# A four-layer image kernel: layer 3 writes its output with channels on partitions, its residual added by an identity product and its shifts as ScalarE's bias

## The chip, the cores and the metric

The kernel runs on one core of a Trainium2 chip. A core has TensorE (PE, with its weight loads PEld), VectorE (DVE), ScalarE (ACT) and GpSimd (POOL), and queues that issue DMAs. The metric is the device time of one execution in microseconds, lower is better. All arithmetic is in float32 except the small bf16 rows named below.

## The reference

The input `x` has 16 images of 64 x 64 tokens and 256 channels. Four layers follow each other, each as `x = x + layer(_gn(x))`, where `_gn` is a group norm over 32 groups of channels:

- Layer 0 replaces each normalized token by the nearest of 1024 code vectors.
- Layer 1 is attention with a sigmoid along each row of the image.
- Layer 2 computes a gate for each token, from a softmax over all pairs of the 4096 tokens of rank-one scores, and multiplies the token by it.
- Layer 3 is linear attention. What matters here is its end:

```python
out = jnp.einsum('bhde,bhdn->bhen', context, q)
...
out = jnp.einsum('bxyh,hc->bxyc', out, w_out) + b_out
mu = jnp.mean(out, axis=-1, keepdims=True)
var = jnp.mean(jnp.square(out - mu), axis=-1, keepdims=True)
out = (out - mu) * jax.lax.rsqrt(var + LN_EPS) * gamma + beta
```

and the sum with the layer's input, which is the result.

## The kernel before, in words

The tokens of an image are worked on in 8 chunks of 512 (`NCHUNK`, `CW`), a chunk being 4 tiles (`CH`) of 128 tokens. Between the layers the activations lie in DRAM with the channels on the partitions: a chunk is 128 partitions x 2 channel halves (`NK`) x 512 tokens.

Each layer is a generator for each image: `stage1` searches the codes, `layer1` is the row attention, `rows2`, `stage2` and `gate2` make layer 2, `stage3` is layer 3. Their steps are merged in an order written out by hand: each stage has a start and a length in units of one image (`LAG4`, `LEN3` for layer 3), and a heap picks the next step. So several images are in flight, each in another layer, and all engines work on all of them. Within that, the scheduler of the language fixes the order on each engine by priority; blocks under `tc.high_priority` are drawn forward.

PSUM is used through two pools: four single banks of 512 columns (`bank`, pool `ps_m`), shared by nearly everything, and two double ones for the search and layer 1.

`stage3` runs over the chunks twice. In the first pass it reads `xk`, makes keys, queries and values (`pk`, `pqv`) and adds up the context; the queries go to DRAM. Then it forms `wctx` from the context, `w_out` and `gamma`. In the second pass each chunk reads its queries back (`fetch`), gets the variance by a product with the Gram matrix (`form`, `variance`), scales the queries by the deviation (`deviate`), and computes the output.

That last step treats a chunk in two halves of two token tiles. For each half a PSUM tile `px` of 128 tokens x 2 x 256 channels takes, in one accumulation, four transposes of the residual `xt` (L902), two products of the scaled queries with `wctx` (L908), and one bf16 product with `x_row` that adds the shifts of each channel to all tokens (L912). ScalarE copies it to `y` (L913), and a chunk's `y` goes out with the tokens on the partitions (L923, L926), in pieces of 256 channels.

The shifts are `xm_`, two columns of 128 channels made in `gate2` (L688: `beta` less the mean that was added there). To add them to tokens on partitions they are needed as a row. `put_row` makes one with a weight function, `by_identity` (L173 to L178): ScalarE copies the column three times (L148), `busy` issues `idle` products that nobody reads (L135), the product with the identity gives a row (L176), and the row is split into three bf16 parts with two more copies, two small products and a last copy (L156 to L158). It is called once an image, in the first chunk of layer 3, with `idle=8` (L789). `h_row` and `qv_row` of layers 1 and 3 are made the same way, without the idle products.

The tag `u4` has two buffers, used by `qv` in the first pass and `y` in the second; `xb` has four, for every chunk that layer 3, `rows2` and the first statistics read.

Of the kernel before, what the change touches and what calls it, by code (L numbers as in the profile page):

```python
# [9 lines left out]
F32 = mybir.dt.float32  # L10
BF16 = mybir.dt.bfloat16
U32 = mybir.dt.uint32
AF = mybir.ActivationFunctionType
# [3 lines left out]
P = 128  # L17
C = 256
NK = C // P
TOK = 4096  # L20
NT = TOK // P
CH = 4
NCHUNK = NT // CH
CW = CH * P
# [19 lines left out]
def kernel(  # L44
# [7 lines left out]
    nc = tc.nc  # L52
# [10 lines left out]
    s3p = ctx.enter_context(tc.tile_pool(name="s3p", bufs=2))  # L63
# [6 lines left out]
    def bank(name):  # L70
        return ps_m.tile([P, 512], F32, tag="pm", name=name)
# [5 lines left out]
    ident = const.tile([P, P], F32, name="ident")  # L77
# [38 lines left out]
    ones3 = const.tile([P, P], BF16, name="ones3")  # L116
# [10 lines left out]
    def row_tile(name):  # L127
        t = const.tile([P, C], BF16, name=name)
        nc.gpsimd.memset(t, 0.0)
        return t  # L130
# [6 lines left out]
                skip_group_check=True,  # L137
            )

    h_row, qv_row, x_row = row_tile("h_row"), row_tile("qv_row"), row_tile("x_row")  # L140

    def twice(row):
        return row.unsqueeze(1).to_broadcast([P, 2, C])

    def put_row(dst, v, weight, tag, plus=None, idle=0):

        v3 = small.tile([P, NK, PARTS], F32, tag="v3", name=f"v3_{tag}")
        nc.scalar.copy(v3, v.unsqueeze(2).to_broadcast([P, NK, PARTS]))  # L148
        pb = bank(f"prow_{tag}")
        busy(pb, idle)  # L150
        row = pb[:PARTS, :C]
        weight(row, v3, plus)

        for n in range(PARTS - 1):
            top = small.tile([PARTS, C], BF16, tag="ptop", name=f"top_{tag}_{n}", bufs=1)
            nc.scalar.copy(top, row)  # L156
            nc.tensor.matmul(row, lhsT=below[:, n, :], rhs=top, start=False, stop=True, skip_group_check=True)
        nc.scalar.copy(dst[0:PARTS, :], row)  # L158

    def by_weight(w):  # L160
# [9 lines left out]
                    skip_group_check=True,  # L170
                )
        return make

    def by_identity(out, v3, plus):
        for k in range(NK):
            nc.tensor.matmul(  # L176
                out[:, k * P : (k + 1) * P], lhsT=v3[:, k, :], rhs=ident, start=(k == 0), stop=(k == NK - 1),
                skip_group_check=True,  # L178
            )


    e_raw = s2p.tile([P, NK, CODES], F32, tag="x0b", name="e_raw", bufs=2)
# [6 lines left out]
    for hf in range(2):  # L189
        pe = bank(f"pe_{hf}")  # L190
        for k in range(NK):
            nc.tensor.matmul(
                pe, lhsT=neg_mat, rhs=e_sq[:, k, hf * 512 : (hf + 1) * 512],
                start=(k == 0), stop=(k == NK - 1),
# [54 lines left out]
    for n in range(2):  # L249
        t = const.tile([P, CH, 2, ROW], F32, name=f"blk_{n}")  # L250
# [4 lines left out]
    for n in range(4):  # L255
        t = const.tile([P, 8], F32, name=f"m8_{n}")
# [459 lines left out]

    def stage3(b):
        tag = f"s3_{b}"
        dst = out[b].rearrange("(t p) c -> p t c", p=P)
        x3 = x3_d.pop(b)  # L720
        scale, nmean, xm_ = norm3.pop(b)
        wk_n = wts.tile([P, NK, P], F32, tag="wk_n", name=f"wk_{tag}")
# [35 lines left out]
        for ch in range(NCHUNK):  # L758
            xt = xb.tile([P, NK, CW], F32, tag="xb", name=f"xk_{tag}_{ch}")
            nc.sync.dma_start(out=xt, in_=x3[ch])  # L760
            if ch > 0:
                normalize(ch - 1)
            pk = bank(f"pk_{tag}_{ch}")
            for k in range(NK):
                nc.tensor.matmul(pk, lhsT=wk_n[:, k, :], rhs=xt[:, k, :], start=(k == 0), stop=(k == NK - 1))  # L765

            now = nkm[:, ch : ch + 1]
            nc.vector.tensor_reduce(now, pk, AX.X, ALU.max, negate=True)
            if ch > 0:
                last = nkm[:, ch - 1 : ch]  # L770
                nc.vector.tensor_scalar(now, now, last, None, ALU.min)
                nc.scalar.activation(al[:, ch : ch + 1], last, AF.Exp, scale=-1.0, bias=now)
            kx = s3p.tile([P, CW], F32, tag="v2", name=f"kx_{tag}_{ch}", bufs=7)
            nc.scalar.activation(kx, pk, AF.Exp, bias=now, accum_out=ks[:, ch : ch + 1])
            qv = s3p.tile([P, CH, 2, P], F32, tag="u4", name=f"qv_{tag}_{ch}")
            qvs[ch] = qv
            for pr in range(CH // 2):
                pqv = bank(f"pqv_{tag}_{ch}_{pr}").rearrange("p (j n) -> p j n", j=2)
                for j in range(2):
                    t = 2 * pr + j  # L780
                    for k in range(NK):
                        nc.tensor.matmul(  # L782
                            pqv[:, j, :], lhsT=xt[:, k, t * P : (t + 1) * P], rhs=wqv_n[:, k, :],
                            start=(j == 0 and k == 0), stop=False, skip_group_check=True,
                        )
                nc.tensor.matmul(pqv, lhsT=ones3, rhs=twice(qv_row), start=False, stop=True, skip_group_check=True)
                nc.scalar.copy(qv[:, 2 * pr : 2 * pr + 2, :, :].rearrange("p j s n -> p j (s n)"), pqv)
            if ch == 0:
                put_row(x_row, xm_, by_identity, f"x_{tag}", idle=8)  # L789
            yield 5  # L790
            pkt = bank(f"pkt_{tag}_{ch}")
            for t in range(CH):
                nc.tensor.transpose(pkt[:, t * P : (t + 1) * P], kx[:, t * P : (t + 1) * P], ident)
            ek = s3p.tile([P, CH, P], F32, tag="v2", name=f"ek_{tag}_{ch}", bufs=7)
            nc.scalar.copy(ek.rearrange("p t d -> p (t d)"), pkt)
            if ch > 0:
                queries(ch - 1)

            q4 = qv[:, :, 0, :].rearrange("p t (h d) -> p t h d", d=DH)
            qm = small.tile([P, CH, HEADS], F32, tag="qm", name=f"qm_{tag}_{ch}")  # L800
            nc.vector.tensor_reduce(qm, q4, AX.X, ALU.max)  # L801
            nc.gpsimd.tensor_tensor(q4, q4, qm.unsqueeze(3).to_broadcast([P, CH, HEADS, DH]), ALU.subtract)  # L802
            nc.scalar.activation(qv[:, :, 0, :], qv[:, :, 0, :], AF.Exp)

            pc = bank(f"pc_{tag}_{ch}")
            for t in range(CH):
                nc.tensor.matmul(pc[:, :P], lhsT=ek[:, t, :], rhs=qv[:, t, 1, :], start=(t == 0), stop=(t == CH - 1))
            if ch > 0:
                nc.vector.scalar_tensor_tensor(
                    ctxa, ctxa, al[:, ch : ch + 1], pc[:, :P], op0=ALU.mult, op1=ALU.add  # L810
                )
            else:
                nc.vector.tensor_copy(ctxa, pc[:, :P])
            yield 5
# [15 lines left out]
        with tc.high_priority(offset=URGENT):  # L830
# [8 lines left out]
            wctx = wts.tile([P, 2, C], F32, tag="wctx", name=f"wctx_{tag}")  # L839
# [50 lines left out]
        for ch in range(NCHUNK):  # L890
            xt = xb.tile([P, NK, CW], F32, tag="xb", name=f"xo_{tag}_{ch}")
            nc.sync.dma_start(out=xt, in_=x3[ch])
            qT = qs[ch]
            y = s3p.tile([P, CH, C], F32, tag="u4", name=f"y_{tag}_{ch}")
            for pr in range(2):
                if pr == 1 and ch + 1 < NCHUNK:
                    deviate(ch + 1)
                px = bank(f"pxo_{tag}_{ch}_{pr}").rearrange("p (j c) -> p j c", c=C)
                for j in range(2):
                    t = 2 * pr + j  # L900
                    for k in range(NK):
                        nc.tensor.matmul(  # L902
                            px[:, j, k * P : (k + 1) * P], lhsT=xt[:, k, t * P : (t + 1) * P], rhs=ident,
                            is_transpose=True, start=(j == 0 and k == 0), stop=False, skip_group_check=True,
                        )
                for j in range(2):
                    t = 2 * pr + j
                    nc.tensor.matmul(  # L908
                        px[:, j, :], lhsT=qT[:, t * P : (t + 1) * P], rhs=wctx[:, 1, :], start=False, stop=False,
                        skip_group_check=True,  # L910
                    )
                nc.tensor.matmul(px, lhsT=ones3, rhs=twice(x_row), start=False, stop=True, skip_group_check=True)  # L912
                nc.scalar.copy(y[:, 2 * pr : 2 * pr + 2, :], px)  # L913
                if pr == 0:
                    if ch + 2 < NCHUNK:
                        form(ch + 2)
                    if ch + 3 < NCHUNK:
                        fetch(ch + 3)
                else:
                    if ch + 2 < NCHUNK:  # L920
                        variance(ch + 2)
                    if before is not None:
                        nc.sync.dma_start(out=dst[:, (ch - 1) * CH : ch * CH, :], in_=before)  # L923
                yield 3
            before = y
        nc.sync.dma_start(out=dst[:, TOK // P - CH :, :], in_=before)  # L926

# [75 lines left out]
```

## Time and profile before

| | us |
|---|---|
| median of 3 runs | 5682.38 (5680.2 to 5684.69) |
| the profiled execution | 5674.06 |
| its span, first to last instruction | 5672.1 |
| busy: PE, PEld | 5162.0, 3189.6 |
| busy: DVE, ACT, POOL | 5049.3, 4571.1, 1801.5 |
| mean granted clock of TensorE | 0.962 |

The span has 76,096 instructions. A line such as `L902 PE MATMUL pxo_s<-ident,xo_s 128*128 128x128 f32` names the line of the kernel, the engine, the operation, the tile written and those read (the program's names, shortened) and the size. A float32 product shows as two records, a transpose or a bf16 product as one. The records of successive matmuls overlap, so that the distance from one start to the next says what a matmul occupies, and its duration says more than that. The DMA lines count packets: 521,365 in the run, with 1059.26 MB.

### The profile page before, as it was taken

What the parts mean: (1) busy time and instruction counts of PE and PEld (TensorE: products, weight loads), DVE (VectorE), ACT (ScalarE), POOL (GpSimd) and SP (SyncE); (2) the same over time, 40 slices, a digit from 0 to 9 for tenths busy, and PEclk for the clock granted to TensorE, in tenths of its full rate; (3) what the DMA queues carried; (4) which work ended last, traced back from release to release, by engine and by line L of the source; (5) the groups of instructions that cost most, each with busy time, mean ns of one, the idle gap of its engine ahead of it and who ended that gap; (6) DMA issues with size and microseconds to landing.
All of it is one profiled execution on the core that took longest, in us unless ns stands there. A gap on an engine that the chain in (4) does not pass through costs nothing.

```text
span 5672.1 us, 76096 instructions
## 1 busy us (share of the span) xinstructions
PE 5162.0 (91%) x26927; PEld 3189.6 (56%) x26927; DVE 5049.3 (89%) x7186; ACT 4571.1 (81%) x6642; POOL 1801.5 (32%) x1076
## 2 busy tenths in 40 slices
PE   7977889989999999999999999999999999987788
PEld 3534446545656566565655656565565656564556
DVE  7589799899999999999999999999999999988882
ACT  4468589888989898888978888898888879887873
POOL 2223234323333333334333333333333333321221
PEclk9988999999999999999999999999999999998889
DMA  8553744655665757566575656657575675745543
GB/s 254 174 178 84 232 115 144 214 163 185 196 198 175 224 159 236 171 211 198 185 234 155 216 185 200 210 173 236 160 224 183 201 219 156 222 149 176 200 157 119
DMA packets 521365, 1059.26 MB, mean 187 GB/s; under 512 B 52504, under 2 KB 266392, under 8 KB 512792
## 3 DMA queue, kind: packets, MB, share of 16 engines
q1 hardware_dynamic: 406288, 885.11, 46.5%
q0 software_dynamic: 73728, 67.14, 8.3%
q10 hardware_dynamic: 40968, 102.13, 4.6%
q8 instruction: 214, 3.51, 0.3%
q14 instruction: 167, 1.37, 0.1%
HBM read 751.18 MB, written 303.04 MB: 186 GB/s over the span
## 4 chain that ended last, share of the span: by engine, by line
PE 46%; DVE 17%; ACT 16%; issue 6%; DMA 5%; POOL 4%; SPq 0%; ACTq 0%; DVEq 0%; POOLq 0%
PE pd_s L403 14%; ACT ex_s L645 7%; DVE ex_s L648 7%; PE ph_l L493 4%; PE pxo_s L908 3%; PE pqv_s L782 3%; PE po_l L533 2%; PE pk_s L765 2%; ACT nn_s L398 2%; POOL qv_s L802 2%; PE pz_s L857 2%; DVE i_s L414 2%; DVE nn_s L409 2%; PE pxo_s L902 2%; PE pvr_s L865 2%
## 5 line engine op out<-in xcount | busy, mean ns | idle before, releaser
L648 DVE CUSTOM_DVE_ANT_0 ex_s<-ex_s,x2b 128x2048 f32<-128x2048 f32 x1024 | 2360.4, 2312 | 77.6 <-ACT ex_s L645 74.6
L645 ACT ACTIVATE ex_s<-x0b,nmax_s,x_r 128x2048 f32<-128x2048 f32 x1024 | 2138.6, 2089 | 40.7 <-DVE num_s L648 30.5
L403 PE MATMUL pd_s<-e,xn_s 128*128 128x512 f32 x4096 | 1971.1, 614 | 43.9 <-DVE m L409 27.9
L415 POOL DMA_INDIRECT xc_s<-in_emb_rows,i_s x512 | 1113.7, 2175 | 1852.7 <-DVE i_s L414 1337.5
L403 PEld LDWEIGHTS pd_s<-e,xn_s 128*128 128x128 f32 x4096 | 745.8, 195 | 778.8 <-issue 669.1
L409 DVE CUSTOM_DVE_ANT_0 nn_s<-pd_s,nn_s 128x1024 f32<-128x1024 f32 x512 | 619.9, 1212 | 113.5 <-PE pd_s L403 63.0
L414 DVE FIND_INDEX8 i_s<-m,nn_s 128x8 uint32<-128x1024 f32 x512 | 622.9, 1217 | 0.0
L398 ACT ACTIVATE nn_s<-ne,nx_s 128x1024 f32<-128x1024 f32 x512 | 582.5, 1143 | 33.1 <-DVE nx_s L369 18.7
L493 PE MATMUL ph_l<-wh_l,xt_l 128*128 128x256 f32 x2048 | 519.6, 390 | 28.7 <-DVE m L409 16.9
L782 PE MATMUL pqv_s<-wqv_s,xk_s 128*128 128x256 f32 x2048 | 489.3, 381 | 0.0
L493 PEld LDWEIGHTS ph_l<-wh_l,xt_l 128*128 128x128 f32 x2048 | 379.7, 192 | 138.9 <-issue 69.0
L782 PEld LDWEIGHTS pqv_s<-wqv_s,xk_s 128*128 128x128 f32 x2048 | 389.1, 191 | 120.6 <-issue 59.7
L802 POOL TENSOR_TENSOR qv_s<-qv_s,qm_s 128x512 f32<-128x512 f32 x128 | 221.6, 1731 | 662.6 <-DVE qm_s L801 363.2
L868 POOL TENSOR_TENSOR lrs_s<-lrs_s,mhalf 128x4 f32<-128x4 f32 x128 | 178.0, 1391 | 677.2 <-ACT lrs_s L867 663.3
L756 POOL TENSOR_TENSOR qv_s<-qv_s,qd_s 128x512 f32<-128x512 f32 x128 | 214.4, 1675 | 249.0 <-DVE qd_s L755 132.0
L533 PE MATMUL po_l<-blk,h_l 128*128 128x128 f32 x2048 | 282.1, 288 | 3.0 <-DVE m L409 1.5
L533 PEld LDWEIGHTS po_l<-blk,h_l 128*128 128x128 f32 x2048 | 260.6, 200 | 41.1 <-issue 24.5
L908 PE MATMUL pxo_s<-wctx_s,qo_s 128*128 128x256 f32 x1024 | 269.2, 386 | 2.2 <-DVE qo_s L876 2.2
L765 PE MATMUL pk_s<-xk_s,wk_s 128*128 128x512 f32 x512 | 256.0, 620 | 1.0 <-DMA xk_s<-x_g 0.9
L913 ACT COPY y_s<-pxo_s 128x512 f32<-128x512 f32 x256 | 147.5, 580 | 132.4 <-PE pxo_s L912 116.0
L378 PE MATMUL pt_s<-ident,xc_s 128*128 128x128 f32 x1024 | 156.7, 282 | 105.2 <-DMA xc_s<-in_emb_rows,i_s 79.0
L351 ACT ACTIVATE sq_s<-xt_s,first 128x512 f32<-128x512 f32 x256 | 200.2, 806 | 37.2 <-DMA x0b<-rows_r 21.0
(206 smaller groups left out, 7322.0 us busy)
## 6 DMA issues: line engine op xcount, KB each, us to landing
xs_s<-in_xT SPq DMA_DIRECT2D x128, 512.0 KB
xt_s<-in_xT SPq DMA_DIRECT2D x128, 512.0 KB
xc_s<-in_x SPq DMA_DIRECT2D x128, 512.0 KB
x_s<-xt_s ACTq DMA_DIRECT2D x128, 512.0 KB
xt_l<-x_s SPq DMA_DIRECT2D x128, 512.0 KB
x_l<-xt_l SPq DMA_DIRECT2D x128, 512.0 KB
xr_r<-x_l SPq DMA_DIRECT2D x128, 512.0 KB
xg_g<-x_l SPq DMA_DIRECT2D x128, 512.0 KB
```

What stands on the lines that cost most here:

```text
L398: nc.scalar.activation(nn, ne2, AF.Identity, bias=nx2[ch][:, t : t + 1])
L403: nc.tensor.matmul(pd[:, cols], lhsT=xn[ch][:, k, t * P : (t + 1) * P], rhs=e2[:, k, cols], start=(k == 0), stop=(k == NK - 1),)
L409: nc.vector.tensor_tensor_reduce(out=nn, in0=pd, in1=nn, scale=1.0, scalar=-3.0e38, op0=ALU.add, op1=ALU.max, accum_out=m8[:, 0:1],)
L414: nc.vector.max_index(i8, m8, nn)
L415: nc.gpsimd.indirect_dma_start(out=xc[ch][:, t, :], out_offset=None, in_=emb_rows, in_offset=bass.IndirectOffsetOnAxis(ap=i8[:, 0:1], axis=0),
L493: nc.tensor.matmul(ph[:, t, :], lhsT=X[:, k, t * P : (t + 1) * P], rhs=wh_n[:, k, :], start=(t % 2 == 0 and k == 0), stop=False, skip_grou ...
L533: nc.tensor.matmul(po[:, m : m + P], lhsT=h[:, t, k * P : (k + 1) * P], rhs=at[:, t, :, :].rearrange("p r i -> p (r i)"), start=True, stop ...
L645: nc.scalar.activation(ex, x0b, AF.Exp, bias=nmax[:, T : T + 1], scale=x01[:, T, 1:2], accum_out=den[:, h, T : T + 1])
L648: nc.vector.tensor_tensor_reduce(out=ex, in0=ex, in1=x2b, scale=1.0, scalar=0.0, op0=ALU.mult, op1=ALU.add, accum_out=num[:, h, T : T + 1],)
L765: nc.tensor.matmul(pk, lhsT=wk_n[:, k, :], rhs=xt[:, k, :], start=(k == 0), stop=(k == NK - 1))
L782: nc.tensor.matmul(pqv[:, j, :], lhsT=xt[:, k, t * P : (t + 1) * P], rhs=wqv_n[:, k, :], start=(j == 0 and k == 0), stop=False, skip_group ...
L908: nc.tensor.matmul(px[:, j, :], lhsT=qT[:, t * P : (t + 1) * P], rhs=wctx[:, 1, :], start=False, stop=False, skip_group_check=True,)
```

## The change

Layer 3's output keeps the channels on the partitions. A half of a chunk is now one of the two channel halves, with all 512 tokens. Its PSUM bank takes one product of the identity with the residual, and one product of a 128-column part of `wctx` with the scaled queries of the whole chunk; ScalarE adds the shifts as a bias of each partition while it copies. `x_row`, its `put_row` call and `by_identity` go. The output tensor is declared in the layout that comes out, 4 KB for each partition and chunk, and the host turns the result round after the run.

```diff
-    h_row, qv_row, x_row = row_tile("h_row"), row_tile("qv_row"), row_tile("x_row")
+    h_row, qv_row = row_tile("h_row"), row_tile("qv_row")
...
-    def by_identity(out, v3, plus):
-        for k in range(NK):
-            nc.tensor.matmul(
-                out[:, k * P : (k + 1) * P], lhsT=v3[:, k, :], rhs=ident, start=(k == 0), stop=(k == NK - 1),
-                skip_group_check=True,
-            )
...
-        dst = out[b].rearrange("(t p) c -> p t c", p=P)
+        dst = out[b].rearrange("c p (k n) -> c p k n", k=NK)
...
-            if ch == 0:
-                put_row(x_row, xm_, by_identity, f"x_{tag}", idle=8)
...
-            y = s3p.tile([P, CH, C], F32, tag="u4", name=f"y_{tag}_{ch}")
-            for pr in range(2):
+            y = s3p.tile([P, NK, CW], F32, tag="u4", name=f"y_{tag}_{ch}")
+            for pr in range(NK):
                 if pr == 1 and ch + 1 < NCHUNK:
                     deviate(ch + 1)
-                px = bank(f"pxo_{tag}_{ch}_{pr}").rearrange("p (j c) -> p j c", c=C)
-                for j in range(2):
-                    t = 2 * pr + j
-                    for k in range(NK):
-                        nc.tensor.matmul(
-                            px[:, j, k * P : (k + 1) * P], lhsT=xt[:, k, t * P : (t + 1) * P], rhs=ident,
-                            is_transpose=True, start=(j == 0 and k == 0), stop=False, skip_group_check=True,
-                        )
-                for j in range(2):
-                    t = 2 * pr + j
-                    nc.tensor.matmul(
-                        px[:, j, :], lhsT=qT[:, t * P : (t + 1) * P], rhs=wctx[:, 1, :], start=False, stop=False,
-                        skip_group_check=True,
-                    )
-                nc.tensor.matmul(px, lhsT=ones3, rhs=twice(x_row), start=False, stop=True, skip_group_check=True)
-                nc.scalar.copy(y[:, 2 * pr : 2 * pr + 2, :], px)
+                px = bank(f"pxo_{tag}_{ch}_{pr}")
+                nc.tensor.matmul(px, lhsT=ident, rhs=xt[:, pr, :], start=True, stop=False)
+                nc.tensor.matmul(px, lhsT=wctx[:, 1, pr * P : (pr + 1) * P], rhs=qT, start=False, stop=True)
+                nc.scalar.activation(y[:, pr, :], px, AF.Identity, bias=xm_[:, pr : pr + 1])
...
-                        nc.sync.dma_start(out=dst[:, (ch - 1) * CH : ch * CH, :], in_=before)
+                        nc.sync.dma_start(out=dst[ch - 1], in_=before)
...
-    o = nc.dram_tensor("out_0", (x.shape[0], TOK, C), F32, kind="ExternalOutput").ap()
+    o = nc.dram_tensor("out_0", (x.shape[0], NCHUNK, P, NK * CW), F32, kind="ExternalOutput").ap()
...
-    return r.results[0]["out_0"].reshape(x.shape)
+    y = r.results[0]["out_0"].reshape(x.shape[0], NCHUNK, P, NK, CW)
+    return y.transpose(0, 1, 4, 3, 2).reshape(x.shape)
```

More of the change, by code (lines that the diff above doesn't have):

```diff
@@ L922, in stage3 @@
                     if before is not None:
-                        nc.sync.dma_start(out=dst[:, (ch - 1) * CH : ch * CH, :], in_=before)
+                        nc.sync.dma_start(out=dst[ch - 1], in_=before)
                 yield 3
             before = y
-        nc.sync.dma_start(out=dst[:, TOK // P - CH :, :], in_=before)
+        nc.sync.dma_start(out=dst[NCHUNK - 1], in_=before)
     tasks, free = [], {}
```

## The prediction

> **What bounds the kernel now.** I read the page's first two parts, then busy time by stretch, then the chain that ended last, and last the groups and the order of time around the edited lines.
>
> ```profile
> PE 5162.0 (91%) x26927; PEld 3189.6 (56%) x26927; DVE 5049.3 (89%) x7186; ACT 4571.1 (81%) x6642; POOL 1801.5 (32%) x1076
> PEclk9988999999999999999999999999999999998889
> ```
>
> TensorE leads, VectorE is two points behind. The mean hides the start and the end, so the stretches decide (columns: us, then busy time of PE, PEld, DVE, ACT and POOL with instruction counts, granted clock, DMA share, GB/s):
>
> ```profile
> 1846.00:4828.00 2982.00, 2816.78 (x15027) 1755.54 (x15028) 2796.20 (x3965) 2542.21 (x3699) 1023.71 (x588) 0.98 0.63 197
> 4970.00:5540.00 570.00, 446.24 (x2343) 317.43 (x2343) 479.50 (x657) 447.16 (x676) 124.98 (x83) 0.87 0.51 171
> 5632.00:5661.00 29.00, 29.00 (x186) 23.91 (x184) 7.13 (x11) 8.55 (x18) 5.08 (x6) 1.00 0.63 201
> ```
>
> In the first row, over half the span, PE is busy 2816.8 of 2982 us, 94.5%; DVE is at 93.8%, ACT at 85%. The last row is layer 3's output loop of the last image, alone on the chip: PE never stops. Only the second row leaves PE slack. The chain agrees:
>
> ```profile
> PE 46%; DVE 17%; ACT 16%; issue 6%; DMA 5%; POOL 4%; SPq 0%; ACTq 0%; DVEq 0%; POOLq 0%
> ```
>
> So a microsecond of PE counts almost fully, one of ACT about a sixth, and a DMA saved counts little.
>
> **The output loop on PE.** There are 16 images x 8 chunks x 2 halves = 256 halves. One of them, back to back at full clock:
>
> ```profile
> 2496.49 0.60 PE L902 MATMUL pxo_s<-ident,xo_s 128*128 128x128 f32 x4
> 2496.92 1.03 PE L908 MATMUL pxo_s<-wctx_s,qo_s 128*128 128x256 f32 x4
> 2497.79 0.38 PE L912 MATMUL pxo_s<-x_row,ones 128*128 128x512 bf16 x1
> 2498.01 0.39 PE L865 MATMUL pvr_s<-one,qz_s 128*128 128x1 f32 x3
> ```
>
> Starts, not durations, give what each step occupies, since matmuls overlap: four transposes 0.43 us, two 256-column f32 products (four records) 0.87, the bf16 row 0.22; together 1.52 us. After the change a half is two f32 products of 512 columns. Their price stands in the trace: the search runs such products in a row,
>
> ```profile
> 2408.65 3.60 PE L403 MATMUL pd_s<-e,xn_s 128*128 128x512 f32 x8
> 2412.09 0.61 PE L533 MATMUL po_l<-blk,h_l 128*128 128x128 f32 x4
> ```
>
> eight records (four products) in 3.44 us, 0.86 each; layer 3's own `pz` costs the same (L857 at 5636.06, next start 5636.91). So a half becomes 1.72 us. The context product keeps its columns (0.87 against 0.86) and the row's 0.22 goes, but the identity product costs 0.86 where the transposes cost 0.43. Net +0.20 us a half, +51.2 us. The saved weight loads (nine records become four) give nothing: PEld is busy 56% and hides behind the products.
>
> [...]
>
> **The row that goes.** `put_row` for `x_row` runs once an image, in layer 3's first chunk:
>
> ```profile
> 839.04 1.89 PE L135 MATMUL prow_x_s<-ones 128*128 128x512 bf16 x8
> 840.86 0.60 PE L176 MATMUL prow_x_s<-ident,v_x_s 128*3 128x128 f32 x4
> 841.39 0.66 PE L793 MATMUL pkt_s<-ident,kx_s 128*128 128x128 f32 x4
> 843.70 0.27 PE L157 MATMUL prow_x_s<-top_x_s,below 3*3 3x256 bf16 x1
> 843.89 1.16 PE L807 MATMUL pc_s<-qv_s,ek_s 128*128 128x128 f32 x8
> 845.84 0.27 PE L157 MATMUL prow_x_s<-top_x_s,below 3*3 3x256 bf16 x1
> ```
>
> The eight idle products take 1.82 us, the row's product 0.53, the two corrections 0.20 each: 2.75 us, x16 = 44.0 us saved. So PE's balance is 51.2 - 44.0 = +7.2 us, not the saving that "nine instructions become two" suggests. I price both sides in full, because PE is 94.5% busy where most of them lie. If only the additions counted it would be +51, if only the savings -44: these ends go into the range. In the last image, alone on PE, the same sum holds: eight chunks x 0.41 us more, 2.75 less.
>
> **ACT.** The copy becomes an activation with a bias per partition; the nearest row is the one Identity with such a bias out of PSUM at this size:
>
> ```profile
> L913 ACT COPY y_s<-pxo_s 128x512 f32<-128x512 f32 x256 | 147.5, 580 | 132.4 <-PE pxo_s L912 116.0 <-issue 12.6 <-DMA out<-y_s 1.0
> L597 ACT ACTIVATE rows_r<-pr_r,brow_r 128x512 f32<-128x512 f32 x32 | 21.8, 682 | 55.3 <-PE pr_r L593 55.3
> ```
>
> 682 - 580 = 0.10 us x 256 = +26.1. The row's ACT work goes: 0.194 (L148) + 2 x 0.349 (L156) + 0.358 (L158) = 1.25 us x 16 = -20.0. Net +6.1 us; at ACT's 16% of the chain, +1.0. Behind a later eviction the next group for the same PSUM bank waits; the page of `y` names such waiters at 0.4 to 15.1 us over the whole run (`pz` the largest), so 0.1 us more on 256 evictions is inside that +1.
>
> **Output DMA.** The bytes are the same; 512 pieces of 1 KB a chunk become 128 of 4 KB, 49,152 of the run's 521,365 packets less. Almost nobody waits for this store (`out<-y_s` ended 2.1 us of waiting in all), and between 1700 and 4900 us PE waited 13.5 us in all on any DMA. [...] SP's issue (0.39 us each) delays nothing on the chain. `y` and `qv` share two buffers as before. The one memset less on POOL lies at the start, off the path.
>
> **DVE** has no instruction changed. `xt` is now read in two wide products instead of eight narrow ones, and freed at the same place, the first step of the second half.
>
> **Sum:** +7.2 + 1.0 + 0 = +8 us on the profiled execution's 5674.06 (span 5672.1), that is 5682. That execution lies 8.3 us below the median 5682.38 of the runs shown, so against the median the forecast is **5690 us**, +0.14%. About 0.2%, 11 us, is what a measurement of this kernel can tell from no change.
>
> **Spread.** The scheduler lays out every engine's order anew when instructions vanish, so waits move far from the edit. What that may be worth shows between images: the first transposition of the context (L832) of each image comes 330.8 to 338.2 us after the one before, in the eight periods between 2110 and 4784 us, for the same work. A standard deviation near 2.5 us over 14 independent periods makes 9 us; a shift of that size shared by all of them makes 35. I take 5658 to 5728.
>
> **Rivals.**
> *The savings were slack (slower).* The idle products and the row's chain sit at layer 3's start; if they fill time in which PE would have waited anyway, nothing comes back and the 51 us remain: 5682 + 51 + 26 x 0.16 = 5738; with half of the row's work being slack, 5682 + 29 + 3 = 5714. For it: `put_row` is a chain of ACT and PE steps around other work, and its fillers need nobody's data. Against: in the lines above PE goes from one to the next without a gap, and list order puts other work between the corrections. Chance 0.27.
>
> *The clock gains (faster).* The granted clock in the long stretch is 0.98, which is 60 us of PE time lost at 2982 us. It falls in short pieces after thin PE activity, for instance when `pz` waits 2 us for `qo`. Wide products in place of narrow steps could keep it up: from 0.987 on (21 us back) this outweighs the +8 by more than the measurement can miss, and 0.99 gives 30 - 8 = 22 us, 5660. [...] Chance 0.23.
>
> [...]
>
> *It does not do what it says:* the output could lose its one-bank groups or its contiguous store. The diff shows both kept, so I give this no chance of its own; a store of small pieces would show in the packets.
>
> **How the numbers follow.** The balance case (+8, order noise of 9 us or more either way) has 0.50: 0.30 of it within 0.2%, 0.16 above, 0.04 below. With the slack rival 0.27 (0.26 slower, 0.01 same) and the clock rival 0.23 (all faster but 0.01) this makes faster 0.26, same 0.32, slower 0.42. The balance case's own range is 5672 to 5708; 5658 to 5728 reaches into both rivals and leaves out their far thirds.
>
> **What would show it.** Right: L902 and L912 gone, two groups of 512 records of 128x512 f32 on `pxo` at 0.43 us from start to start, no `prow_x`; PE busy up by about 7 us; the `y` activation near 680 ns; 4 KB packets, about 49,000 packets less; the last image's chunk pitch 5.17 to 5.58 us. Wrong: a `y` activation at 580 or 800 ns, a 512-column identity product cheaper than 0.86 us, a clock of 0.99 or 0.97 in the long stretch, or a DVE busy share that falls while PE's stays: then the order, not the price, moved the time.

## The result, and the profile after

The kernel after takes 5728.05 us (median of 4 runs, 5722.48 to 5731.14) against 5681.29 us for the kernel before in the same comparison (5678.33 to 5684.69). The ratio is 1.0081, with a 95% interval of 1.0064 to 1.0098: **47 us slower**, at the very end of the range (5728), where the likeliest case had +8.

Busy time and the clock by slices, from the page:

```profile
span 5726.5 us, 73048 instructions
PE 5190.7 (91%) x25423; PEld 3051.9 (53%) x25423; DVE 5044.1 (88%) x7186; ACT 4574.6 (80%) x6578; POOL 1810.8 (32%) x1075
PEclk9988999999999999999999999999999999998989
DMA packets 472201, 1059.06 MB, mean 185 GB/s; under 512 B 52505, under 2 KB 200857, under 8 KB 463641
```

The span grew by 54.4 us. PE's busy time grew by 28.7 of these, and the time in which PE does nothing (span less busy) by the other 25.7, from 510.1 to 535.8. DVE has the same work and 59.6 us more of idle time. 49,164 packets are gone.

Then the groups of the edited lines (busy time in us, mean ns of one, idle time before them):

```profile
L890 PE MATMUL pxo_s<-xo_s,ident 128*128 128x512 f32 x512 | 271.1, 611 | 0.0
L891 PE MATMUL pxo_s<-qo_s,wctx_s 128*128 128x512 f32 x512 | 263.0, 595 | 0.0
L892 ACT ACTIVATE y_s<-pxo_s,xm_g 128x512 f32<-128x512 f32 x256 | 174.2, 682 | 126.3 <-PE pxo_s L891 108.3
```

and their order of time in the last image, which runs alone on the chip (start, duration):

```profile
5689.22 1.02 PE L890 MATMUL pxo_s<-xo_s,ident 128*128 128x512 f32 x2
5690.08 1.02 PE L891 MATMUL pxo_s<-qo_s,wctx_s 128*128 128x512 f32 x2
5690.94 0.95 PE L856 MATMUL pvr_s<-one,qz_s 128*128 128x1 f32 x8
```

From 5689.22 to 5690.94 is 1.72 us for a half, as the prediction had it, and the activation takes its 682 ns. The prices of the edit are right. One chunk of this loop takes 5.62 us, where 5.58 was forecast and 5.17 stood before. Busy time by stretch comes next: the two stretches that the prediction showed, and a part of the last image's output loop in place of the third:

```profile
1846.00:4828.00 2982.00, 2803.42 (x13940) 1658.58 (x13939) 2743.23 (x3904) 2502.49 (x3605) 1021.65 (x582) 0.98 0.62 194
4970.00:5540.00 570.00, 452.97 (x2151) 290.65 (x2150) 506.54 (x694) 469.66 (x695) 128.29 (x90) 0.89 0.52 175
...
5686.00:5715.00 29.00, 29.00 (x115) 16.49 (x115) 6.44 (x10) 8.65 (x17) 5.21 (x6) 1.00 0.59 197
```

In the long stretch PE's share fell from 94.5% to 94.0% and DVE's from 93.8% to 92.0%: in the same time every engine gets less done. The loss is spread over the whole run: the period from one image's context transposition to the next, which the prediction used for its spread, is 337.7 us on average over ten images, where it was 332.3, and each of the ten is longer. The chain of waits says the same in another way, PE a point less, DVE two points more:

```profile
PE 45%; DVE 19%; ACT 15%; issue 6%; DMA 6%; POOL 3%; SPq 0%; ACTq 0%; DVEq 0%; POOLq 0%
```

The waits of PE show one place, far from layer 3, where it lost time (total us, times, longest). First before, then after:

```profile
PE pg_n L285 <- DVE mv_n L281: 41.2, 24, 11.0
```

```profile
PE pg_n L278 <- DVE mv_n L274: 66.2, 25, 11.6
PE pd_s L396 <- DVE m L402: 39.8, 25, 6.0
```

`pg_n` is the product of the group norm, here that of layer 0's output at the end of each image's search. In the two traces, four search products of the next image (eight records) stand between the last transposes and `pg_n` in seven of the later images before, and two (four records) after. These seven waits make 0.6 us before and 25.9 after, all that this wait grew by. The order of time on PE at one of these places, before and then after:

```profile
2984.02 3.60 PE L403 MATMUL pd_s<-e,xn_s 128*128 128x512 f32 x8
2987.45 0.28 PE L285 MATMUL pg_n<-mv_n,dmat 128*128 128x2 f32 x2
```

```profile
3021.61 1.88 PE L396 MATMUL pd_s<-e,xn_s 128*128 128x512 f32 x4
3026.86 0.56 PE L278 MATMUL pg_n<-mv_n,dmat 128*128 128x2 f32 x2 [3.36 <-DVE mv_n L274]
...
3029.87 1.92 PE L396 MATMUL pd_s<-e,xn_s 128*128 128x512 f32 x2
```

Before, eight records of the search cover the time that DVE needs for `mv_n`. After, four do, PE stands still for 3.36 us, and what follows runs at half speed: the search products last 1.92 us and not 1.02. In the clock's records the time at half speed is 429 us of the run before and 480 after.

The same traces hold a reason for doubt. In the first three of the ten periods `pg_n` stands behind eight records after and six before, and doesn't wait at all after (1.6 us in all before). Yet these periods are 8.0, 3.4 and 5.1 us longer, 5.5 on average, as much as the seven with the wait (38.2 us in all). One of the three places, before and then after:

```profile
1986.71 2.74 PE L403 MATMUL pd_s<-e,xn_s 128*128 128x512 f32 x6
1990.15 0.35 PE L285 MATMUL pg_n<-mv_n,dmat 128*128 128x2 f32 x2 [0.70 <-DVE mv_n L281]
```

```profile
2005.18 3.60 PE L396 MATMUL pd_s<-e,xn_s 128*128 128x512 f32 x8
2008.62 0.28 PE L278 MATMUL pg_n<-mv_n,dmat 128*128 128x2 f32 x2
```

### The profile page after: what moved, and what is told of

Read it like the earlier page. It is cut to its first block, busy times and chain, and to the rows that moved or that the text cites. A ratio compares the mean times of both kernels' runs of the same rounds, so it can differ in the third digit from the quotient of the medians.

```text
span 5726.5 us, 73048 instructions
## 1 busy us (share of the span) xinstructions
PE 5190.7 (91%) x25423; PEld 3051.9 (53%) x25423; DVE 5044.1 (88%) x7186; ACT 4574.6 (80%) x6578; POOL 1810.8 (32%) x1075
## 3 DMA queue, kind: packets, MB, share of 16 engines
q1 hardware_dynamic: 357136, 885.11, 46.0%
## 4 chain that ended last, share of the span: by engine, by line
PE 45%; DVE 19%; ACT 15%; issue 6%; DMA 6%; POOL 3%; SPq 0%; ACTq 0%; DVEq 0%; POOLq 0%
PE pd_s L396 13%; DVE ex_s L641 8%; ACT ex_s L638 7%; PE ph_l L486 4%; PE pxo_s L890 3%; PE pxo_s L891 3%; DVE i_s L407 3%; PE pqv_s L775 2%; PE po_l L526 2%; PE pk_s L758 2%; ACT nn_s L391 2%; DVE nn_s L402 2%; PE pz_s L848 2%; POOL qv_s L793 2%; PE pvr_s L856 2%
## 5 line engine op out<-in xcount | busy, mean ns | idle before, releaser
L641 DVE CUSTOM_DVE_ANT_0 ex_s<-ex_s,x2b 128x2048 f32<-128x2048 f32 x1024 | 2356.6, 2309 | 87.6 <-ACT ex_s L638 85.0
L396 PE MATMUL pd_s<-e,xn_s 128*128 128x512 f32 x4096 | 1990.4, 619 | 52.8 <-DVE m L402 39.8
L408 POOL DMA_INDIRECT xc_s<-in_emb_rows,i_s x512 | 1148.9, 2244 | 1840.6 <-DVE i_s L407 1316.8
L402 DVE CUSTOM_DVE_ANT_0 nn_s<-pd_s,nn_s 128x1024 f32<-128x1024 f32 x512 | 619.6, 1212 | 122.0 <-PE pd_s L396 81.2
L486 PE MATMUL ph_l<-wh_l,xt_l 128*128 128x256 f32 x2048 | 523.3, 392 | 28.6 <-DVE m L402 24.4
L749 POOL TENSOR_TENSOR qv_s<-qv_s,qd_s 128x512 f32<-128x512 f32 x128 | 188.6, 1473 | 333.2 <-DVE qd_s L748 177.6
L892 ACT ACTIVATE y_s<-pxo_s,xm_g 128x512 f32<-128x512 f32 x256 | 174.2, 682 | 126.3 <-PE pxo_s L891 108.3
L890 PE MATMUL pxo_s<-xo_s,ident 128*128 128x512 f32 x512 | 271.1, 611 | 0.0
L891 PE MATMUL pxo_s<-qo_s,wctx_s 128*128 128x512 f32 x512 | 263.0, 595 | 0.0
```

Of the source, the lines that this page charges most:

```text
L396: nc.tensor.matmul(pd[:, cols], lhsT=xn[ch][:, k, t * P : (t + 1) * P], rhs=e2[:, k, cols], start=(k == 0), stop=(k == NK - 1),)
L402: nc.vector.tensor_tensor_reduce(out=nn, in0=pd, in1=nn, scale=1.0, scalar=-3.0e38, op0=ALU.add, op1=ALU.max, accum_out=m8[:, 0:1],)
L408: nc.gpsimd.indirect_dma_start(out=xc[ch][:, t, :], out_offset=None, in_=emb_rows, in_offset=bass.IndirectOffsetOnAxis(ap=i8[:, 0:1], axis=0),
L486: nc.tensor.matmul(ph[:, t, :], lhsT=X[:, k, t * P : (t + 1) * P], rhs=wh_n[:, k, :], start=(t % 2 == 0 and k == 0), stop=False, skip_grou ...
L641: nc.vector.tensor_tensor_reduce(out=ex, in0=ex, in1=x2b, scale=1.0, scalar=0.0, op0=ALU.mult, op1=ALU.add, accum_out=num[:, h, T : T + 1],)
L890: nc.tensor.matmul(px, lhsT=ident, rhs=xt[:, pr, :], start=True, stop=False)
```

## The experiments

Three theories were put against each other. The *work theory*: time follows PE's microseconds, each at its full price. The *slack theory*, the rival on record: the row's products filled time in which PE waits anyway. The *order theory*: taking instructions out makes the scheduler lay out every engine's order anew, and the waits that come with the new order are the cost. Ratios are against the kernel before, run beside each kernel on the same chip (its medians there: 5679.57, 5677.78 and 5681.97 us). The ratios as recorded differ from the quotients of these medians by up to 0.001, and by 0.003 with GpSimd, so a difference of some 5 us between kernels says nothing.

**The row made again, unread, in the kernel after.** `put_row` is called as before, and nothing reads the row.

```diff
+            if ch == 0:
+                put_row(x_row, xm_, by_identity, f"x_{tag}", idle=8)
```

> The kernel after, with the row of the shifts made again as before (eight idle products, the row's product, two corrections, five copies), though nothing reads it. Work theory (every microsecond of PE counts, in whichever kernel): 44 us more PE than after, so 5728 + 44 = 5772. Slack theory (the row's work lay in time in which PE waited): 5728, no change. Order theory (taking the row away let the scheduler place layer 0's group-norm product behind two search products instead of four, so that PE waits some 3.4 us for VectorE and then runs 6.8 us at half clock, in seven to ten images): the order is the one of before again, four products; that wait goes, the work is paid, so before's 5681 + 51 (PE) + 4 (ACT) = 5736, and the 3.4 us waits of PE for mv_n are gone.

Measured: 5697.67 us, ratio 1.0034 (1.0019 to 1.0048). By the prices this kernel has 44 us more work on PE than the kernel after, and it is 30 us faster; `pg_n` waits 41.3 us for `mv_n` again. Against the kernel before, it has +51 us on PE and costs +19. At both steps the work theory is far off, and the other two missed as well (5728 and 5736 were expected): eight search records stand ahead of `pg_n` again in the seven images, but the time is 38 us below what the order theory made of that. It looks like a proof that the row's idle products help; whether it is one is for the experiment with the order alone.

**The kernel before without the idle products.**

```diff
-                put_row(x_row, xm_, by_identity, f"x_{tag}", idle=8)
+                put_row(x_row, xm_, by_identity, f"x_{tag}", idle=0)
```

> The kernel before, with idle=0 for the row of the shifts: only the eight idle products of each image go, 29 us of PE. Work theory: 5681 - 29 = 5652. Slack theory: 5681. Order theory: the number of search products ahead of layer 0's group-norm product falls from four to two in seven images as in the kernel after, so PE waits for mv_n there and the clock drops, 5 to 7 us each: 5652 + 40 = 5692 or about the time of before, with the waits of PE for mv_n near 66 us instead of 41.

Measured: 5706.27 us, ratio 1.0050 (1.0033 to 1.0068). 29 us of products that nobody reads are gone (16 x 1.82 us), and the time is 27 us longer, above what any of the three theories gave (5692 at most). `pg_n` waits 64.6 us for `mv_n`, with four records ahead of it in the seven images, as the order theory had it.

**Idle products alone in the kernel after, 8 or 12 of them at the row's place.**

```diff
+            if ch == 0:
+                busy(bank(f"idle_{tag}"), 8)
```

> The kernel after, with eight idle products put at the place where the row of the shifts was, without the row. By the list of instructions, layer 0's group-norm product then stands behind no search product at all in seven images (two in after, four in before). Work theory: 5728 + 29 = 5757. Slack theory: 5728. Order theory: the worst of the set, 5757 + 7 x 1.7 = 5769, with PE's waits for mv_n above after's 66 us.

> The same with twelve idle products; by the list of instructions the group-norm product then stands behind three search products in seven images. Work theory: 5728 + 44 = 5772, slower than with eight. Slack theory: 5728. Order theory: faster than with eight although it has more work, 5728 + 44 - 25 = 5747, with PE's waits for mv_n below after's.

Measured: with 8 5708.29 us, ratio 1.0059 (1.0039 to 1.0078); with 12 5698.31, ratio 1.0038 (1.0017 to 1.0060). Both are faster than the kernel after, with more work, and both lie 20 us or more below all three theories (5728 to 5772). Between the two, the intervals overlap. But `pg_n`'s wait was 72.2 us with 8 of them, more than after, and the time was still 20 us shorter: that one wait doesn't carry the time.

**The place itself, by order of issue alone.** In the kernel after, the two products of that group norm are queued behind the first or the second tile of the next image's search (four or eight search products). No work changes.

```diff
+                        searched[b, T] = nc.tensor.matmul(
...
+        if b + 1 < nb:
+            yield 4.5
+        with ExitStack() as queued:
+            queued.enter_context(tc.high_priority(offset=URGENT))
+            if b + 1 < nb:
+                queued.enter_context(tc.issue_after(getattr(searched[b + 1, 0], "ins", searched[b + 1, 0])))
-        with tc.high_priority(offset=URGENT):
```

(8.5 and `searched[b + 1, 1]` for the second tile.)

> The kernel after with no work added or taken: the products of layer 0's group norm of an image are queued on PE behind the first tile of the next image's search, so that transposes and products of layer 3 that are ready stand ahead of the product that waits for VectorE. Work theory and slack theory: 5728, no change. Order theory: PE's waits for mv_n fall from 66 us to near 41 as in the kernel before, the slow pieces of the clock fall from 480 us toward 430, and the time goes to 5728 - 25 - 25 = 5680 at best, 5695 if other waits take half of it.

> The same, queued behind the second tile of the next image's search: one step more of other work ahead of the product. Work and slack theories: 5728. Order theory: waits for mv_n at this place gone, time as with the first tile or 5 us better or worse, since layer 1 of the image starts about 2 us later.

Measured: 5719.9 us, ratio 1.0077 (1.0053 to 1.0100), and 5707.54, ratio 1.0049 (1.0024 to 1.0074). The wait for `mv_n` falls to 48.6 and 36.8 us, and at best 20 of the 47 us come back, where up to 48 were expected; the first kernel can't be told from the one after. With the second tile PE's idle time is 545.3 us, more than the 535.8 after: other waits came in, such as 35.4 us of `ph_l` for DVE's `m`, 24.4 in the kernel after. The two waits there:

```profile
PE pg_n L278 <- DVE mv_n L274: 36.8, 16, 11.8
PE ph_l L492 <- DVE m L403: 35.4, 20, 3.1
```

The wait found in the profile was at most a part of the cost, not its cause.

**What a microsecond of PE is worth.** The identity product in bf16, on the upper halves of the residual's words: its lower 16 bits are left out.

```diff
+    ident_b = const.tile([P, P], BF16, name="ident_b")
+    nc.vector.tensor_copy(ident_b, ident)
...
-                nc.tensor.matmul(px, lhsT=ident, rhs=xt[:, pr, :], start=True, stop=False)
+                high = xt[:, pr, :].bitcast(BF16).rearrange("p (n h) -> p n h", h=2)[:, :, 1]
+                nc.tensor.matmul(px, lhsT=ident_b, rhs=high, start=True, stop=False)
```

> The kernel after with the identity product in bf16 on the upper halves of the residual's words, so the residual is added with its lower 16 bits left out. A product falls from 0.86 to 0.22 us, 0.64 x 256 = 164 us of PE less. Work theory with every microsecond of PE counted: 5728 - 164 = 5564. Order theory: a microsecond of PE is worth about a third (the kernel with the row made again paid 18 us for 51 more on PE than before), 5728 - 55 = 5673, moved by some 25 us either way by the new order. Slack theory: the additions count in full, 5564 as well.

Measured: 5706.77 us, ratio 1.0061 (1.0036 to 1.0087). The product in the order of time, and the page:

```profile
5669.45 0.39 PE L894 MATMUL pxo_s<-xo_s,ident_b 128*128 128x512 bf16 x1
5669.67 1.02 PE L851 MATMUL pz_s<-qo_s,gram_s 128*128 128x512 f32 x2
```

```profile
PE 5082.9 (89%) x25167; PEld 3006.0 (53%) x25167; DVE 5044.1 (88%) x7187; ACT 4576.2 (80%) x6578; POOL 1830.4 (32%) x1075
```

A product is now 0.22 us from start to start where it was 0.86, 164 us less for the 256 halves, and the time is 21 us less; the order theory's 5673, give or take 25, is missed too. PE's busy time fell by 108 us only (5190.7 to 5082.9), its idle time rose by 87 (535.8 to 622.4), and the time at half clock went from 480 to 545.

**The residual by GpSimd.** No identity product; GpSimd adds the residual to `y`.

```diff
-                nc.tensor.matmul(px, lhsT=ident, rhs=xt[:, pr, :], start=True, stop=False)
...
+                nc.gpsimd.tensor_tensor(y[:, pr, :], y[:, pr, :], xt[:, pr, :], ALU.add)
```

> The kernel after without the identity product: GpSimd adds the residual to y in SBUF after ScalarE's activation, 256 additions of 128x512, at some 1.5 to 1.7 us each by GpSimd's rows 400 us more on an engine that is busy 32%; PE loses 0.86 x 256 = 220 us. Work theory: 5728 - 220 = 5508, or VectorE's limit. Order theory: a third of it, 5728 - 73 = 5655, and less if the gathers of layer 0 wait for GpSimd.

Measured: 5798.15 us, ratio 1.0238 (1.0186 to 1.0289). The adds, as a group:

```profile
L892 POOL TENSOR_TENSOR y_s<-y_s,xo_s 128x512 f32<-128x512 f32 x256 | 422.5, 1652 | 470.6 <-ACT y_s L891 467.1 <-ACT d_n L281 2.3 <-DMA out<-y_s 1.1
```

220 us of PE's work are gone and the kernel is 70 us slower than the one after by the medians, where the order theory had 5655 and the work theory 5508. GpSimd has 422 us more, and half clock rises to 740 us; which of the two cost the time, or whether the order did, is not shown.

**An order laid anew with no work changed.** This asks what a new order is worth by itself. `LAG4` is the start of layer 3 in units of an image; 0.01 of it is about 3.3 us. The kernel after with layer 3 later and sooner, and the kernel before with it sooner:

```diff
-LAG4 = 0.04
+LAG4 = 0.05
```

> The kernel after, with the due time of layer 3 put back by 0.01 of an image (0.04 to 0.05, about 3.3 us); every instruction's work is the same, only the order of issue is laid anew. Order theory (what the removal of the row cost comes from the re-laid order, waits of PE for VectorE above all): the time moves by 10 to 30 us, either way, PE busy stays at 5160 to 5200 us, and the time follows PE's waits and the slow-clock time. Rival (the idle products of the row helped where they stood, by keeping the clock up or by holding back what follows): nothing of that is put back, so 5728 within 5 us.

> The kernel after, with the due time of layer 3 put forward by 0.01 of an image (0.04 to 0.03, about 3.3 us); no work changed. Order theory: the time moves by 10 to 30 us, either way; here the group norm's product stands directly behind the last transposes, with no search product between, so PE's waits for mv_n are expected at 70 us or more and the time at 5730 to 5750. Rival (idle products): 5728 within 5 us.

> The kernel before, with the due time of layer 3 put forward by 0.01 of an image; no work changed, the row and its idle products stand. Order theory: 5665 to 5710, away from 5680 by about as much as the change itself moved the time. Rival (idle products, which are all here): 5680 within 5 us.

Measured: after, later: 5758.34 us, ratio 1.0145 (1.0125 to 1.0165). After, sooner (0.03): 5748.97, ratio 1.0133 (1.0112 to 1.0155). Before, sooner: 5752.42, ratio 1.0134 (1.0114 to 1.0153). The kernel before loses 70 us to a nudge of 3.3 us that removes nothing and adds nothing, more than the change cost, and more than I expected (up to 5710). Busy time in the steady part, 1450 to 4850 us, of the kernel before and then of the nudged one:

```profile
1450.00:4850.00 3400.00, 3219.70 (x17230) 2008.13 (x17229) 3190.23 (x4516) 2914.23 (x4233) 1171.04 (x670) 0.99 0.63 196
```

```profile
1450.00:4850.00 3400.00, 3158.11 (x16785) 1979.28 (x16787) 3112.27 (x4407) 2839.67 (x4131) 1169.90 (x656) 0.97 0.62 192
```

It is the picture of the change, only larger: PE and DVE both less busy, the clock lower, 445 matmul records fewer in the same time. The waits of PE that grew here are for the most part others than those of the change:

```profile
PE pt_s L378 <- DMA xc_s<-in_emb_rows,i_s: 109.4, 41, 8.6
PE pg_n L285 <- DVE mv_n L281: 49.9, 22, 12.7
PE pwt_s L845 <- DVE wctx_s L840: 49.0, 14, 6.0
PE pt_s L378 <- ACT kx_s L774: 38.6, 8, 5.4
```

`pwt_s` waited 8.4 us before, `pt_s` for its DMA 79.0, `pg_n` 41.2. In these runs each new order has its waits at other places. For `e9_sooner` I expected `mv_n` to be the carrier again, with 70 us or more; it was 58.3, and 54.3 us of `pgt_s` waiting for `gate_s` had come in, 9.2 in the kernel after.

**The pinned order in the kernel before.** The edit that helped the kernel after most, behind the second tile, made in the kernel before.

> The kernel before, with the two group norm products of each image's layer 0 output queued behind the second tile of the next image's search (order of issue alone). Order theory: PE's waits for mv_n fall from 41 to 37 us or lower, and the time is 5660 to 5680 if no other wait is laid in its place; in the kernel after the same edit gave 20 us. Rival (the place of that product does not matter where four search products already lie ahead of it): 5680 within 5 us.

Measured: 5672.76 us, ratio 0.9982 (0.9968 to 0.9997), the only kernel here below the one before, by 10 us, about the least that can be told from no change. The wait for `mv_n` is 37.0 us. Of the twelve kernels, the order theory's figures held in three (layer 3 later and sooner in the kernel after, and this one): it names the term, but did not give its size.

## Why the prediction was right or wrong

**The two families.** Three edits of the order now stand with and without the change:

| order | without the change | with it | change in the ratio |
|---|---|---|---|
| as given | 1 | 1.0081 | +0.0081, 46 us |
| `pg_n` behind the second tile | 0.9982 | 1.0049 | +0.0067, 38 us |
| layer 3 sooner by 0.01 | 1.0134 | 1.0133 | -0.0001, -1 us |

The intervals of the last two differences are about 17 us either way (the half widths of their two ratios, added in squares). The same change is worth -1 to +46 us, depending on the order that it lands in. A pair does not share one order, though: the change lays it anew under each edit too. The kernels with the work of the one after run from 5707.54 to 5758.34 us (five of them), those with the work of the one before from 5672.76 to 5752.42 (three).

**Prices: right.** A half costs 1.72 us, the activation 682 ns, the row and L902, L912 are gone, the packets fell as forecast, and the loop's 29 us in the last image have PE busy throughout at a clock of 1.00. No run shows the sum's 0 for the output's packets by itself; the packets of the queue that lost them took 46.5% of the 16 DMA engines' span before and 46.0% after, for the same 885.11 MB, and PE waited 13.5 and 9.5 us for any DMA between 1700 and 4900 us. Of the 28.7 us that PE's busy time grew by, 7.2 is the balance of 51.2 and -44.0. The rest is of the size that half clock gives, as an estimate: at half speed a search product held PE for 1.71 us where one at full clock takes 0.86 (3029.87 in the trace of the kernel after), so 51 us more of it can stretch busy time by up to 25. But PE's busy time also differs by 23 us between the kernel before and its nudged form with the same instructions, so that this split is an estimate, not a measurement.

**"A microsecond of PE counts almost fully": the step that failed.** Without 164 us of PE's work the kernel gained 21 us. At full price it should have been at 5564. Kernels of the same work differ by up to 51 us with the work of the one after and by up to 80 with that of the one before, and neither covers the 143 that are missing. As an estimate from these few orders, a microsecond of PE was worth at most (21 + 80) / 164 = 0.62 here. The prediction's own chain gave PE 46%; it priced ACT by its share of that chain, 16%, and PE at one. A busy share of 94.5% beside one of 93.8% is not one engine that bounds and one that follows: in the page after, the search products of PE wait 39.8 us for DVE's `m`, and DVE's step on them (L402) waits 81.2 us for the products. What was taken from PE came back as waiting (+87 us) and as busy time that did not fall (56 us of the 164). By the same estimate the 65 us more at half clock can explain up to 33 of these 56, but half clock also rose by 110 us in the kernel after and by 150 in the kernel before when only layer 3's start was moved sooner. That pricing gave both terms of the sum, 51.2 and -44.0; that they nearly cancel is why the failure did little harm to their sum.

**The spread: right in kind, too small in size.** The prediction named the new order as a cost of its own and took 9 us for it in its likeliest case, from the scatter of the periods in one run, with a shift of 35 us as the outer case. Periods of one order say little about another order: they share its waits. The nudges moved the time by 30 and 21 us (after) and 70 us (before). Its sign for wrong, "a DVE busy share that falls while PE's stays", is nearly what the long stretch shows (93.8 to 92.0% beside 94.5 to 94.0%). That the new order made up the 39 us beyond the +8 is argued from this sign and from the size of the nudges; no run shows it directly. And that the time lies just at the end of the range is luck: one nudge of the kernel after passes it by 30 us.

**The rival of slack: near by number, not shown in its reason.** 5728 lies in its 5714 to 5738. But slack would make the row free to put back and its eight idle products free to take out, and these edits moved the time by -30 and +27 us. Nor do they show the opposite, that the fillers help where they stand: in a kernel that has all of them, a nudge that touches none costs 70 us. Neither the 19 us between the kernel before and the one with the row made again, nor the 30 between that and the kernel after, is the price of an edit.

**The rival of the clock: the gain did not come.** The clock fell from 0.962 to 0.958 over the run; it was 0.963 with the row made again, 0.952 and 0.936 where 164 and 220 us of PE's work were gone, and 0.950 in the kernel before with its order nudged. In the trace of the kernel before, the drops after a wait for `qo` are there: `pz` waits 2.00 us for it up to 2854.56 and 2.04 up to 3190.35, and the clock is 0.50 from 2856.31 and from 3190.81, for 3.4 us each. But 1024 transposes went and the clock did not rise, and with the order's own effect on it the runs can't tell what wide products in place of narrow steps do to it by themselves. The output loop of the last image shows no loss by the residual's transposes, at 1.00 over 29 us with them and without, but products fill most of its time (the transposes 0.43 of the 1.52 us of a half).

**What stays open.** Which waits make up the loss beyond the 20 us that the second tile brought back, and what the work of the change costs without an order of its own. Three pairs give -1 to 46 us; the +8 lies inside and is not shown. A rival is left, too: the kernel before has an order written out by hand, and this order may be a favourable one. Of the two nudges of that kernel one cost 70 us and one gained 10; if most other orders are slower, nearly any edit would lose, whatever its work. A clean price would need many orders of both kernels.

## What to carry to other kernels

Where a scheduler lays the order and two engines are both busy nearly all the time (94.5 and 93.8% in the long stretch here), treat "the order is laid anew" as a term of its own, and size it by nudging a due time in the kernel before, not by the scatter inside one run: here it was worth 10 to 70 us, against 8 us of work. Before a removal or an addition is called good or bad, run it in two or three orders; the same change cost 46, 38 and -1 us. And price work by the wait that it ends, not by the share of a busy engine: 164 us less on the busiest engine gave 21.

## What was not expected of the hardware

- The stop of PE shown above cost twice. After the 3.36 us without work that end at 3026.86, the search product that starts at 3029.87 holds PE until 3031.58, 1.71 us where one at full clock takes 0.86; the clock's record has half speed from 3026.5 to 3033.3. Time at half speed, 429 us in the kernel before, was 545 where 164 us of PE's work went and 740 where 220 did. It does not follow PE's work alone: with layer 3 sooner by 0.01 it was 579 in the kernel before and 590 in the kernel after.
- GpSimd's add of 128x512 f32 took 1.65 us on average (median 1.28), and beside 256 of them DVE was busy for 5120.5 us, where the thirteen other kernels have 5028.7 to 5062.0 for the same DVE work but for one copy. Two of DVE's groups make up 61 us of it against the kernel after: each of 1024 `ex_s` (L641) took 2355 ns and not 2309, each of 256 `xg_g` (L696) 867 and not 817. No run here shows what made them longer.
